# Graph stage: mask, shift, comparison and outputs as products of 32 columns, the centre's share as three bf16 parts

## The chip, the cores and the metric

One core of a Trainium2 chip runs the kernel. It has a matrix engine (TensorE, PE in the profile; its weight loads are PEld), VectorE (DVE), ScalarE (ACT), GpSimd (POOL) and SyncE (SP), which issues the DMAs. The metric is the device time of one execution in microseconds (us), as the median of several runs.

## What is computed

The reference is one layer of a small perceiver: a point cloud network over a context, whose result is added to `x`, a state space layer ("scan"), and a low rank feed forward layer. The change touches the first. For each of 16 batches there are 512 nodes with 32 features, ordered in four ways along space filling curves. In each order a node has a window of K = 10 neighbours. What matters here, cut from the reference:

```python
def _get_graph_features(feats, inds_list, perm, W_lin, b_lin, k=K):
    ...
    for inds in inds_list:
        neigh = gather(feats, inds)
        gf = jnp.concatenate([jnp.broadcast_to(center, (B, N, k, C)), neigh - center], axis=-1)
    ...
    x16 = x.astype(jnp.float16).astype(jnp.float32)
    qh = x16.reshape(B * N, k, nheads, headdim)
    scores = jnp.einsum('bihd,bjhd->bhij', qh, qh) / np.float32(np.sqrt(headdim))
    attn = jax.nn.softmax(scores, axis=-1)
    out = jnp.einsum('bhij,bjhd->bihd', attn, qh).reshape(B * N, k, total)
    fused = out @ W_lin.T + b_lin
...
g1 = _get_graph_features(f0, inds_list, perm1, W_lin1, b_lin1)
h1 = _lrelu(_instance_norm(jnp.einsum('oc,bnkc->bonk', W_conv1, g1), (2, 3)))
feats1 = h1.max(axis=-1)
g2 = _get_graph_features(feats1.transpose(0, 2, 1), inds_list, perm2, W_lin2, b_lin2)
h2 = _lrelu(_instance_norm(jnp.einsum('oc,bnkc->bonk', W_conv2, g2), (2, 3)))
feats2 = h2.max(axis=-1)
```

Layer 1 has 32 output channels, layer 2 has 64. The centre's half of the features is the same for all ten rows of a window, so its share of the output is one vector per node (`hc`), added to what attention gives of the differences to the neighbours.

## The kernel before

The kernel has three stages one behind the other: the graph stage (`graph_part`), the scan and the feed forward layer. The graph stage first makes the space filling keys and the first ranks, then runs eight blocks, `order` at L1026: four groups of four batches (128 partitions: four batches by 32 channels), each in layer 1 and in layer 2, as (group, layer) = (0,1), (1,1), (0,2), (2,1), (1,2), (3,1), (2,2), (3,2). A block has 43 iterations of 12 nodes, 344 in all. Layer 1 has one output tile of 128 partitions (`npair` 1), layer 2 two (`npair` 2).

The order of the instructions in this stage is written out by hand (`manual_schedule`, and the loop at L1074), as a pipeline over iterations. In iteration `it` TensorE receives, in this order:

- `expo` of the iteration before: a product of the identity `idb` with the negated row maxima `c` ("shift", L870), which adds to the scores in PSUM; ScalarE then takes the exponential (L875).
- `scores`: first the mask, a product of `mL` and `mR` that opens the accumulation in the PSUM tile `s` (L846), then 16 products of 32 columns (L853).
- perhaps a rank step: `compare`, a product of 128 columns by 512 (L540), whose signs ScalarE sums (L541). There are 256, 64 of them before the blocks, 64 each in the first, second and fourth block.
- `mapped`: 48 products of 32 columns by 128 (layer 1) or 256 (layer 2) that apply the weights, three bf16 parts of them (L915); ScalarE copies the result to `us` (L920).
- perhaps a step of `prep` for the next block, of which the largest on TensorE is `place`, twelve products of 32 columns by 512 (L705), 16 times per block.
- `outputs` of three iterations before: 16 f32 products that apply the attention weights `e` to `us` (L943). Each has `co` columns, 32 in layer 1 and 64 in layer 2; an f32 product is two instructions on TensorE, and every product has a weight load of its own. They go to the PSUM tile `h`, of which there is one buffer; it gathers four iterations in layer 1 and two in layer 2. In layer 1 a first f32 product of the identity and `hc` (L933) puts the centre's share in.

VectorE receives `turn` (a transpose, L896), `rest` and `reduce` (maximum and moments of `h`, L966 and L969; in layer 2 after an add of the centre's share at L960, which also frees `h`, with part of the reductions put off to the next iteration as `rest`), `greatest` (row maxima, L862), `sums` (L882), the one-hot rows of `prep` (L751) and the reciprocal in `shares` (L888). GpSimd makes the differences to the neighbours six iterations ahead (L811) and multiplies by the reciprocal (L890). SyncE issues the copies of those differences (`DX`, L821) and the loads and stores of `prep`.

`prep` is a generator, advanced by `steps` once or twice per iteration while the block before runs; `PREP` is the number of steps it is taken to have. Within it `share` makes `hc`: f16 rounding of the features, an f32 product per output tile (L666), and a copy with bias on ScalarE (L667).

Of the kernel before, what the change touches and what calls it, by code (L numbers as in the profile page):

```python
# [8 lines left out]
F32 = mybir.dt.float32  # L9
F16 = mybir.dt.float16  # L10
BF16 = mybir.dt.bfloat16
I32 = mybir.dt.int32
AF = mybir.ActivationFunctionType
ALU = mybir.AluOpType
AX = mybir.AxisListType
# [3 lines left out]
P = 128  # L19
B = 16  # L20
C = 32
D = 512
NBG = 4
M = 4
K = 10
NG = 12
NGRP = -(-D // NG)
NB = 3
QB = NB * K
NJ = NG // NB  # L30
NI = NJ * 4
# [14 lines left out]
NHT = 16  # L46
LR = 18
LEAD = 6
PREP = (49, 46, 42)
SPARE = 3  # L50


# [325 lines left out]
def graph_part(nc, tc, cx, I, dram, id32, ones, xt, F0, layernorm_steps, rstd_steps, scan_input):  # L378
# [10 lines left out]
    start = ExitStack()  # L389
# [14 lines left out]
    for L, co in ((1, 32), (2, 64)):  # L404
        for n, shape in (("wlA", [64, P]), ("wlC", [64, P]), ("wcT", [64, co]), ("bl", [64, 1])):
            t = wp.tile(shape, F32, name=f"{n}{L}")
            nc.sync.dma_start(out=t, in_=I[f"{n}{L}"])
            loaded[n, L] = t
    for dst, v, at in ((own, -1.0, (0, 4)), (others, 1.0, (2, 7))):
        t = kp.tile([M * B, D], BF16, name=f"sign{at[0]}")  # L410
# [12 lines left out]
    layers = []  # L423
# [8 lines left out]
    for k in range(2):  # L432
        kl = keep.tile([P, M, D], BF16, name=f"kl{k}")
# [23 lines left out]
    NQ = NG * K  # L457
# [21 lines left out]
    nc.scalar.copy(idb, id32)  # L479
    nid = kp.tile([P, P], BF16, name="nid")  # L480
    nc.scalar.mul(nid, id32, -1.0)
    orders = node_orders(nc, kp, kt, kps, X, idx, id32, nid, own, others)


# [52 lines left out]
    def compare(t, b, c, m):  # L537

        kl, kr = KS[b % 2]
        nc.tensor.matmul(t, lhsT=kl[:, m, c * P:(c + 1) * P], rhs=kr, start=True, stop=True)  # L540
        nc.scalar.activation(sgn, t, AF.Sign, accum_out=rank[:, c, m, b:b + 1])  # L541

    ranked = [0]
# [83 lines left out]
    def prep(g, layer, early=False):  # L627
# [26 lines left out]
        def share():  # L654

            c16 = wk.tile([P, D], F16, tag="c16", name=f"c16{key}", bufs=1)
            nc.vector.tensor_copy(c16, src)
            yield
            c32 = wk.tile([P, D], F32, tag="c32", name=f"c32{key}", bufs=1)
            nc.vector.tensor_copy(c32, c16)  # L660
            yield
            yield
            hc = wk.tile([P, npair, D], F32, tag="hc", name=f"hc{key}")
            for pr in range(npair):
                ph = ps_1.tile([P, D], F32, tag="misc", bufs=2, name=f"ph{key}_{pr}")
                nc.tensor.matmul(ph, lhsT=WC[:, pr], rhs=c32, start=True, stop=True)  # L666
                nc.scalar.activation(hc[:, pr], ph, AF.Identity, bias=HB)  # L667
                yield
            made[key][2] = hc

# [170 lines left out]
    def scores(at, gi):  # L841

        slot, c1 = at_piece(at, gi)
        d, dx = DD[slot], DX[slot]
        s = ps_s.tile([P, 512], F32, tag="s", name=f"s{at}_{gi}")[:, :NI * QB]
        nc.tensor.matmul(  # L846
            s, lhsT=mL.rearrange("p i q -> p (i q)"), rhs=mR, start=True, stop=False, skip_group_check=True
        )
        for j in range(NJ):
            c0 = c1 + j * QB  # L850
            for h in range(4):
                rh = slice(32 * h, 32 * h + 32)
                nc.tensor.matmul(  # L853
                    s[rh, j * 4 * QB:(j + 1) * 4 * QB].rearrange("p (b q) -> p b q", b=4),
                    lhsT=d[:, h, c0:c0 + 32], rhs=dx[:, h, :, c0:c0 + QB],
                    start=False, stop=(j == NJ - 1), skip_group_check=True,
                )
        live["s", at, gi] = s
# [8 lines left out]
    def expo(at, gi):  # L867

        s, c = live.pop(("s", at, gi)), live.pop(("c", at, gi))
        nc.tensor.matmul(  # L870
            s, lhsT=idb, rhs=c.unsqueeze(2).to_broadcast([P, NI, QB]), start=False, stop=True,
            skip_group_check=True,
        )
        e = sm.tile([P, NI, QB], F32, tag="e1", name=f"e1{at}_{gi}", bufs=3)
        nc.scalar.activation(e, s.rearrange("p (i q) -> p i q", q=QB), AF.Exp, scale=smc)  # L875
        live["e1", at, gi] = e
# [46 lines left out]
    def outputs(at, gi):  # L923
        key, co, npair, WA, hc, per = state[at][:6]
        us, e = live.pop(("us", at, gi)), live.pop(("e2", at, gi))
        slot = gi % per
        if slot == 0:
            live["h", at] = ps_1.tile([P, npair, per * NQ], F32, tag="h", name=f"h{at}_{gi}")
            if npair == 1:

                f0 = gi * NG
                nn = min(f0 + per * NG, D) - f0
                nc.tensor.matmul(  # L933
                    live["h", at][:, 0, :nn * K].rearrange("p (n j) -> p n j", j=K), lhsT=id32,
                    rhs=hc[:, 0, f0:f0 + nn].unsqueeze(2).to_broadcast([P, nn, K]), start=True, stop=False,
                    skip_group_check=True,
                )
        h = live["h", at]
        for j in range(NJ):
            for b in range(4):  # L940
                pr, r = divmod(b * co, P)
                q0 = slot * NQ + j * QB
                nc.tensor.matmul(  # L943
                    h[r:r + co, pr, q0:q0 + QB], lhsT=us[:, j, b * co:(b + 1) * co],
                    rhs=e[:, 4 * j + b, :QB], start=npair > 1, stop=True, skip_group_check=True,
                )
        if slot == per - 1 or gi == NGRP - 1:
            live["full", at, gi] = h

    def reduce(at, gi):  # L950
        key, co, npair, WA, hc, per, mxo, stats = state[at]
        h = live.pop(("full", at, gi), None)
        if h is None:
            return
        f0 = (gi - gi % per) * NG
        nn = min((gi + 1) * NG, D) - f0
        hs = h[:, :, :nn * K].rearrange("p r (n j) -> p r n j", j=K)
        if layers[order[at][1]][0] == 2:
            t = sm.tile([P, npair, per * NG, K], F32, tag="hs", name=f"hs{at}_{gi}", bufs=1)
            nc.vector.tensor_tensor(  # L960
                t[:, :, :nn], hs, hc[:, :, f0:f0 + nn].unsqueeze(3).to_broadcast([P, npair, nn, K]), ALU.add,
            )
            hs = t[:, :, :nn]

        def greatest_of():
            nc.vector.tensor_reduce(mxo[:, :, f0:f0 + nn], hs, AX.X, ALU.max)  # L966

        def moments(pr):
            nc.vector.bn_stats(stats[:, pr, gi // per], hs[:, pr].rearrange("p n j -> p (n j)"))  # L969

        if npair == 1:
            greatest_of()
            moments(0)
        else:
            moments(0)
            live["rest", at] = lambda: (greatest_of(), moments(1))
        if gi == NGRP - 1:
            rest(at, gi)
            tails.append(end(at))

    def rest(at, gi):
        if ("rest", at) in live:
            live.pop(("rest", at))()

    def end(at):

# [24 lines left out]
    def finish(g, F2):  # L1011
        p3 = ps_1.tile([P, D], F32, tag="misc", bufs=2, name=f"p3_{g}")
        for j, f in enumerate((F0[:, g], F1[g], *F2)):
            nc.tensor.matmul(p3, lhsT=W3[:, j], rhs=f, start=(j == 0), stop=(j == 3))
        h3 = wk.tile([P, D], F32, tag="h3", name=f"h3_{g}", bufs=1)
        nc.scalar.copy(h3, p3)
        yield
        n3 = wk.tile([P, D], F32, tag="n3", name=f"n3_{g}", bufs=1)
        yield from layernorm_steps(sm, n3, h3, f"f{g}")
        yield  # L1020
        nc.vector.scalar_tensor_tensor(n3, n3, 0.2, n3, ALU.mult, ALU.max)
        yield
        nc.vector.tensor_tensor(xt[:, g], xt[:, g], n3, ALU.add)
# [50 lines left out]
    for it in range(len(blocks) + 5):  # L1074

        def do(step, lag):
            if 0 <= it - lag < len(blocks):
                step(*blocks[it - lag])

        at, gi = blocks[it] if it < len(blocks) else (len(order), 0)  # L1080
        if gi == 0 and it < len(blocks):
            begin(at)
        do(expo, 1)
        for oh, of in transfers:
            nc.scalar.dma_start(out=oh, in_=of)
        transfers.clear()
        do(turn, 3)
        do(scores, 0)
        do(rest, 5)
        do(reduce, 4)  # L1090
        if ranked[0] < wanted(at):
            rank_step(later_tile)
        do(greatest, 0)
        do(mapped, 0)
        do(sums, 1)
        if at + 1 == len(order) and gi == 4:
            tails.extend(scan_input(sm, junk(q), q) for q in range(NBG - 1))
        steps(at, gi)
        do(shares, 1)
        if ranked[0] < wanted(at) and (at == 0 or gi % 2):  # L1100
            rank_step(later_tile)
        do(outputs, 3)
        if at == 0 and gi < 8:
            rank_step(later_tile)
        if it + LEAD < len(blocks):
            to, g2 = blocks[it + LEAD]
            if g2 == 0:
                for _ in ahead[to][0]:
                    pass
            differences(to, g2)  # L1110
# [551 lines left out]
```

## Time and profile before

| | us |
|---|---|
| median of 3 runs | 2316.69 (2315.12 to 2320.33) |
| span of the profiled execution | 2316.7 |
| stage before the blocks | 0 to 93.8 |
| layer 1 blocks (first, second, fourth, sixth) | 155.9, 142.6, 146.5, 144.7 |
| layer 2 blocks (third, fifth, seventh, eighth) | 153.8, 153.8, 151.3, 144.6 |
| scan and feed forward, from the end of the last block | about 1030 |

A block is counted from the first mask product (L846) of its first iteration to that of the next block. The lines below are from the list of instruction groups with shapes kept apart: line, engine, operation, tiles written and read, shape and count, then busy us and mean ns of one, then idle time of the engine ahead of them and what ended it.

```profile
L943 PE MATMUL h<-e,us 128*64 128x30 f32 x5504 | 194.3, 223 | 9.6 <-DVE hs L960 6.1 <-DVE e L896 2.7 <-issue 0.3
...
L870 PE MATMUL s<-c,idb 128*128 128x480 bf16 x344 | 130.4, 379 | 5.6 <-DVE c L862 2.7 <-DVE e L896 1.5 <-DVE z L882 0.8
L846 PE MATMUL s<-mR,mL 128*128 128x480 bf16 x344 | 127.0, 369 | 0.0
L705 PE MATMUL pp<-oh,F 128*32 128x512 bf16 x1536 | 109.5, 380 | 3.4 <-ACT so L712 1.5 <-issue 1.1 <-DVE oh L751 0.6
L540 PE MATMUL kd<-kr,kl 128*128 128x512 bf16 x256 | 104.6, 424 | 4.8 <-DMA kr<-others 1.0 <-ACT sgn L541 0.5 <-issue 0.3
...
L943 PE MATMUL h<-e,us 128*32 128x30 f32 x5504 | 84.9, 197 | 21.7 <-issue 13.7 <-DVE e L896 7.4
...
L960 DVE TENSOR_TENSOR hs<-h,hc 128x480 f32<-128x480 f32 x84 | 53.3, 635 | 14.1 <-PE h L943 14.1
```

In a product's form, 128*32 means 128 rows and 32 columns of the array; 128x480 is what moves through it. The mean of one product is its latency, since products run into each other; for what one costs, starts have to be compared. "issue" names idle time for which the profile shows no other engine.

### The profile page before, as it was taken

The page shows a single profiled execution, that of the slowest core. Times are in us where ns is not written, and L with a number is a line of the kernel's source. Part 1 is how long each engine was busy: PE and PEld are TensorE (multiplying, and loading weights), DVE is VectorE, ACT ScalarE, POOL GpSimd, SP SyncE. Part 2 cuts the span into 40 slices and gives each one's busy share as a digit, 9 for nine tenths or more (in the row PEclk, how much of TensorE's full clock was granted, in tenths as well). Part 3 has the DMA queues.
Part 4 walks back from the last instruction along what each step waited for, and adds up shares of the span by engine and source line. Part 5 has one row for each costly group of instructions (what it writes and reads, how often), then busy time and mean ns, then how long its engine had stood idle before and what let it go on. Part 6 is the DMA issues. An engine that isn't in the chain of part 4 may idle for free. (4 is left out here: it accounts for less than half of the span.)

```text
span 2316.7 us, 89754 instructions
## 1 busy us (share of the span) xinstructions
PE 2131.8 (92%) x39522; PEld 1300.3 (56%) x39522; DVE 1835.5 (79%) x3974; ACT 1140.4 (49%) x2073; POOL 840.7 (36%) x897
## 2 busy tenths in 40 slices
PE   5599899999999998899999789989999999999979
PEld 2255555776557775567777544455646566464422
DVE  8488897999989999889999763788786967866643
ACT  6686667556675554455555222433353534435321
POOL 2156656455565565655655100111120202112200
PEclk9899999999999999999999799999999999999989
DMA  1324242231232322323212112112122121211100
GB/s 46 81 59 84 52 81 60 52 83 45 63 76 48 82 52 49 84 47 77 56 36 44 49 51 79 60 56 89 45 73 64 46 91 55 73 60 46 37 37 18
DMA packets 121629, 138.05 MB, mean 60 GB/s; under 512 B 18398, under 2 KB 79506, under 8 KB 121154
## 3 DMA queue, kind: packets, MB, share of 16 engines
q1 hardware_dynamic: 121240, 132.32, 22.5%
q8 instruction: 311, 5.10, 1.0%
q14 instruction: 78, 0.64, 0.1%
HBM read 77.02 MB, written 12.85 MB: 39 GB/s over the span
## 5 line engine op out<-in xcount | busy, mean ns | idle before, releaser
L890 POOL TENSOR_TENSOR EN<-e,rz 128x480 f32<-128x480 f32 x344 | 342.5, 996 | 499.4 <-DVE rz L888 410.2
L915 PE MATMUL u<-WA,DD 128*32 128x128 bf16 (+1 forms) x16512 | 414.1, 248 | 16.6 <-issue 16.4
L920 ACT COPY us<-u 128x512 f32<-128x512 f32 x516 | 302.1, 587 | 152.3 <-PE u L915 136.9
L915 PEld LDWEIGHTS <-DD 128*32 128x32 f16 x16512 | 338.6, 97 | 50.6 <-issue 48.1
L875 ACT ACTIVATE e<-s,smc 128x480 f32<-128x480 f32 x344 | 227.7, 662 | 252.6 <-PE s L870 222.0
L811 POOL TENSOR_TENSOR DD<-fs,crep 128x480 f16<-128x480 f32 (+2 forms) x344 | 349.6, 1017 | 0.0
L943 PEld LDWEIGHTS h<-e,us 128*32 128x32 f32 (+1 forms) x11008 | 246.0, 125 | 133.4 <-issue 66.6
L943 PE MATMUL h<-e,us 128*32 128x30 f32 (+1 forms) x11008 | 279.2, 210 | 31.3 <-issue 14.0
L1368 POOL TENSOR_TENSOR ssq<-ssq,sq 128x512 f32<-128x512 f32 x56 | 89.9, 1606 | 592.6 <-ACT sq L1367 592.6
L862 DVE TENSOR_REDUCE c<-s 128x16 bf16<-128x480 f32 x344 | 220.5, 641 | 83.8 <-PE s L853 80.4
L1181 PE MATMUL ppg<-hT,wing 128*128 128x512 f32 x512 | 238.3, 609 | 0.0
L1181 PE MATMUL ppch<-hT,winch 128*128 128x512 f32 x512 | 230.5, 592 | 0.0
L896 DVE STREAM_TRANSPOSE e<-EN 128x512 f32<-128x512 f32 x344 | 224.7, 653 | 0.0
L882 DVE TENSOR_REDUCE z<-e 128x16 f32<-128x480 f32 x344 | 219.6, 638 | 0.5 <-ACT e L875 0.4
L1194 DVE SCALAR_TENSOR_TENSOR cyh<-ppch,t_conv_w,cyh 128x496 f32<-128x496 f32 (+2 forms) x192 | 137.5, 716 | 99.9 <-ACT cyh L1188 95.3
L541 ACT ACTIVATE sgn<-kd 128x512 bf16<-128x512 f32 x256 | 153.1, 598 | 51.4 <-PE kd L540 48.3
L853 PEld LDWEIGHTS <-DD 128*32 128x32 f16 x5504 | 80.8, 96 | 158.2 <-issue 135.5
L751 DVE TENSOR_SCALAR oh<-it,rank 128x512 bf16<-128x512 f16 x512 | 155.8, 365 | 8.5 <-PE pp L705 8.5
L853 PE MATMUL s<-DX,DD 128*32 128x120 f16 x5504 | 142.3, 221 | 18.6 <-DMA DX<-DD 15.3
L1181 PEld LDWEIGHTS ppch<-hT,winch 128*128 128x128 f32 x512 | 94.5, 190 | 109.1 <-issue 102.5
L1181 PEld LDWEIGHTS ppg<-hT,wing 128*128 128x128 f32 x512 | 94.5, 192 | 107.0 <-issue 99.4
L870 PE MATMUL s<-c,idb 128*128 128x480 bf16 x344 | 130.4, 379 | 5.6 <-DVE c L862 2.7
(372 smaller groups left out, 3156.1 us busy)
## 6 DMA issues: line engine op xcount, KB each, us to landing
DX<-DD SPq DMA_DIRECT2D x456, 90.0 KB
wing<-in_in_proj SPq DMA_DIRECT2D x64, 256.0 KB
winch<-in_in_proj SPq DMA_DIRECT2D x64, 256.0 KB
wo<-in_out_proj SPq DMA_DIRECT2D x64, 256.0 KB
crep<-dC SPq DMA_DIRECT2D x128, 64.0 KB
dS<-so SPq DMA_DIRECT2D x32, 256.0 KB
fs<-dS SPq DMA_DIRECT2D x128, 64.0 KB
wincB<-in_in_proj SPq DMA_DIRECT2D x8, 256.0 KB
```

Of the source, the lines that this page charges most:

```text
L751: nc.vector.tensor_scalar(oh[:, j], it2, rank[:, c, m, 4 * g + b:4 * g + b + 1], None, ALU.is_equal)
L811: nc.gpsimd.tensor_tensor(d[:, :, m0 - n0:n1 - n0], win, crep[:, :, m0:n1].unsqueeze(3).to_broadcast([P, 4, n1 - m0, K]), ALU.subtract,)
L853: nc.tensor.matmul(s[rh, j * 4 * QB:(j + 1) * 4 * QB].rearrange("p (b q) -> p b q", b=4), lhsT=d[:, h, c0:c0 + 32], rhs=dx[:, h, :, c0:c0 ...
L862: nc.vector.tensor_reduce(c, live["s", at, gi].rearrange("p (i q) -> p i q", q=QB), AX.X, ALU.max, negate=True)
L875: nc.scalar.activation(e, s.rearrange("p (i q) -> p i q", q=QB), AF.Exp, scale=smc)
L882: nc.vector.tensor_reduce(z, e, AX.X, ALU.add)
L890: nc.gpsimd.tensor_tensor(en[:, :, :QB], e, rz.unsqueeze(2).to_broadcast([P, NI, QB]), ALU.mult)
L896: nc.vector.transpose(e.rearrange("p i q -> p (i q)"), en.rearrange("p i q -> p (i q)"))
L915: nc.tensor.matmul(u[rh, jj], lhsT=d[:, h, c0:c0 + 32], rhs=WA[k][:, h].rearrange("p b o -> p (b o)"), start=(jj == 0 and k == 0), stop=(k ...
L920: nc.scalar.copy(us[:, j - jj:j + 1], u)
L943: nc.tensor.matmul(h[r:r + co, pr, q0:q0 + QB], lhsT=us[:, j, b * co:(b + 1) * co], rhs=e[:, 4 * j + b, :QB], start=npair > 1, stop=True, ...
L1181: nc.tensor.matmul(pp, lhsT=w[:, k], rhs=hT[:, k], start=(k == 0), stop=(k == 3))
```

## The change

Four products of the whole width become four products of 32 columns each, in a helper `bands`: the comparison, the mask, the shift, and the centre's share. The outputs of layer 2 become twice as many products of 32 columns in place of 64. The centre's share enters `h` by TensorE in both layers, as three bf16 parts in place of one f32 product; the parts are made in `share` by ScalarE and GpSimd. In layer 2 the add on VectorE falls away, the reductions read `h` in PSUM, and all of them stand in `reduce`; `rest` is gone. `PREP` follows the number of steps; three work tiles share buffers with others.

```diff
-PREP = (49, 46, 42)
+PREP = (52, 52, 42)
...
+    def bands(t, lhs_of, rhs, start, stop):
+
+        for r in range(4):
+            rr = slice(32 * r, 32 * r + 32)
+            nc.tensor.matmul(t[rr], lhsT=lhs_of(r, rr), rhs=rhs, start=start, stop=stop, skip_group_check=True)
...
     def compare(t, b, c, m):
-        nc.tensor.matmul(t, lhsT=kl[:, m, c * P:(c + 1) * P], rhs=kr, start=True, stop=True)
+        bands(t, lambda r, rr: kl[:, m, c * P + 32 * r:c * P + 32 * r + 32], kr, True, True)
...
-            c32 = wk.tile([P, D], F32, tag="c32", name=f"c32{key}", bufs=1)
+            c32 = wk.tile([P, D], F32, tag="FT", name=f"c32{key}", bufs=1)
...
-            hc = wk.tile([P, npair, D], F32, tag="hc", name=f"hc{key}")
+            hc = wk.tile([P, 3, npair, D], BF16, tag="hc", name=f"hc{key}")
             for pr in range(npair):
                 ph = ps_1.tile([P, D], F32, tag="misc", bufs=2, name=f"ph{key}_{pr}")
                 nc.tensor.matmul(ph, lhsT=WC[:, pr], rhs=c32, start=True, stop=True)
-                nc.scalar.activation(hc[:, pr], ph, AF.Identity, bias=HB)
+                whole = wk.tile([P, D], F32, tag="whole", name=f"whole{key}_{pr}", bufs=1)
+                nc.scalar.activation(whole, ph, AF.Identity, bias=HB)
+                yield
+                for k in range(3):
+                    nc.scalar.copy(hc[:, k, pr], whole)
+                    if k < 2:
+                        nc.gpsimd.tensor_tensor(whole, whole, hc[:, k, pr], ALU.subtract)
+                        yield
                 yield
...
-        nc.tensor.matmul(
-            s, lhsT=mL.rearrange("p i q -> p (i q)"), rhs=mR, start=True, stop=False, skip_group_check=True
-        )
+        bands(s, lambda r, rr: mL[:, r], mR, True, False)
...
-        nc.tensor.matmul(
-            s, lhsT=idb, rhs=c.unsqueeze(2).to_broadcast([P, NI, QB]), start=False, stop=True,
-            skip_group_check=True,
-        )
+        bands(s, lambda r, rr: idb[:, rr], c.unsqueeze(2).to_broadcast([P, NI, QB]), False, True)
...
-            if npair == 1:
-
-                f0 = gi * NG
-                nn = min(f0 + per * NG, D) - f0
-                nc.tensor.matmul(
-                    live["h", at][:, 0, :nn * K].rearrange("p (n j) -> p n j", j=K), lhsT=id32,
-                    rhs=hc[:, 0, f0:f0 + nn].unsqueeze(2).to_broadcast([P, nn, K]), start=True, stop=False,
-                    skip_group_check=True,
+            f0 = gi * NG
+            nn = min(f0 + per * NG, D) - f0
+            for k in range(3):
+                bands(
+                    live["h", at][:, :, :nn * K].rearrange("p r (n j) -> p r n j", j=K), lambda r, rr: idb[:, rr],
+                    hc[:, k, :, f0:f0 + nn].unsqueeze(3).to_broadcast([P, npair, nn, K]), k == 0, False,
                 )
         h = live["h", at]
         for j in range(NJ):
-            for b in range(4):
-                pr, r = divmod(b * co, P)
-                q0 = slot * NQ + j * QB
+            q0 = slot * NQ + j * QB
+            for o in range(0, 4 * co, 32):
+                pr, r = divmod(o, P)
                 nc.tensor.matmul(
-                    h[r:r + co, pr, q0:q0 + QB], lhsT=us[:, j, b * co:(b + 1) * co],
-                    rhs=e[:, 4 * j + b, :QB], start=npair > 1, stop=True, skip_group_check=True,
+                    h[r:r + 32, pr, q0:q0 + QB], lhsT=us[:, j, o:o + 32],
+                    rhs=e[:, 4 * j + o // co, :QB], start=False, stop=True, skip_group_check=True,
                 )
...
-        if layers[order[at][1]][0] == 2:
-            t = sm.tile([P, npair, per * NG, K], F32, tag="hs", name=f"hs{at}_{gi}", bufs=1)
-            nc.vector.tensor_tensor(
-                t[:, :, :nn], hs, hc[:, :, f0:f0 + nn].unsqueeze(3).to_broadcast([P, npair, nn, K]), ALU.add,
-            )
-            hs = t[:, :, :nn]
...
+        nc.vector.tensor_reduce(mxo[:, :, f0:f0 + nn], hs, AX.X, ALU.max)
+        for pr in range(npair):
             nc.vector.bn_stats(stats[:, pr, gi // per], hs[:, pr].rearrange("p n j -> p (n j)"))
...
-        do(rest, 5)
```

More of the change, by code (lines that the diff above doesn't have):

```diff
@@ L957, in reduce @@
         hs = h[:, :, :nn * K].rearrange("p r (n j) -> p r n j", j=K)
-        if layers[order[at][1]][0] == 2:
-            t = sm.tile([P, npair, per * NG, K], F32, tag="hs", name=f"hs{at}_{gi}", bufs=1)
-            nc.vector.tensor_tensor(
-                t[:, :, :nn], hs, hc[:, :, f0:f0 + nn].unsqueeze(3).to_broadcast([P, npair, nn, K]), ALU.add,
-            )
-            hs = t[:, :, :nn]
-        def greatest_of():
-            nc.vector.tensor_reduce(mxo[:, :, f0:f0 + nn], hs, AX.X, ALU.max)
-        def moments(pr):
-            nc.vector.bn_stats(stats[:, pr, gi // per], hs[:, pr].rearrange("p n j -> p (n j)"))
[L971 to L976, printed above, removed]
+        nc.vector.tensor_reduce(mxo[:, :, f0:f0 + nn], hs, AX.X, ALU.max)
+        for pr in range(npair):
+            nc.vector.bn_stats(stats[:, pr, gi // per], hs[:, pr].rearrange("p n j -> p (n j)"))
         if gi == NGRP - 1:
-            rest(at, gi)
             tails.append(end(at))
-    def rest(at, gi):
-        if ("rest", at) in live:
-            live.pop(("rest", at))()
     def end(at):
@@ L1017, in finish @@
         yield
-        n3 = wk.tile([P, D], F32, tag="n3", name=f"n3_{g}", bufs=1)
+        n3 = wk.tile([P, D], F32, tag="lr", name=f"n3_{g}", bufs=1)
         yield from layernorm_steps(sm, n3, h3, f"f{g}")
```

## The prediction

> **What bounds the kernel now.** I read the engines' busy shares first, then the same shares for each of the eight blocks of the graph stage, then TensorE's timeline inside one layer 2 block and one layer 1 block, then the DMA queues and the stalls of TensorE that no other engine ends. The chain of waits only followed the run's last 87 us, far behind the change, so it says nothing here.
>
> ```profile
> PE 2131.8 (92%) x39522; PEld 1300.3 (56%) x39522; DVE 1835.5 (79%) x3974; ACT 1140.4 (49%) x2073; POOL 840.7 (36%) x897
> ...
> q8 instruction: 311, 5.10, 1.0%
> ```
>
> TensorE leads. The queue line matters more than its 1.0% suggests: 5.10 MB over TensorE's 2 x 39522 instructions is 64.5 bytes each, so q8 is TensorE's own program arriving, 311 packets of 16.4 KB, about 256 instructions (128 pairs of weight load and product) in each.
>
> ```profile
> 392.30:546.10 153.80, 150.85 (x4416) 115.38 (x4414) 144.16 (x342) 83.22 (x140) 87.24 (x96) 0.99 0.27 60
> ...
> 846.40:991.10 144.70, 118.08 (x4444) 75.81 (x4442) 130.37 (x301) 59.16 (x100) 86.94 (x97) 0.96 0.28 63
> ```
>
> The columns are the stretch, its length, and busy us of TensorE, weight loads, VectorE, ScalarE and GpSimd, then clock and DMA. The first row is a layer 2 block: TensorE busy 150.85 of 153.80 us. The second is the layer 1 block without comparisons: only 118.08 of 144.70. A steady layer 2 iteration:
>
> ```profile
> 1103.65 0.38 PE L870 MATMUL s<-c,idb 128*128 128x480 bf16 x1
> 1103.87 0.37 PE L846 MATMUL s<-mR,mL 128*128 128x480 bf16 x1
> 1104.16 0.40 PE L853 MATMUL s<-DX,DD 128*32 128x120 f16 x16
> 1104.39 1.48 PE L915 MATMUL u<-WA,DD 128*32 128x256 bf16 x48
> 1105.80 1.12 PE L943 MATMUL h<-e,us 128*64 128x30 f32 x32
> 1106.86 0.38 PE L870 MATMUL s<-c,idb 128*128 128x480 bf16 x1
> ```
>
> From start to start: shift 0.213, mask 0.296, scores 0.229, map 1.416, outputs 1.056, in all 3.21 us (three digits are medians over all iterations). Each step between widths costs: the map takes 1.309 us ahead of other 32 column products and 1.416 ahead of the 64 column outputs; the scores take 0.229 ahead of the map and 0.337 ahead of a comparison; mask to scores is 0.296 and shift to mask 0.213. So narrowing the array costs about 0.085 us and widening 0.105 us. That is what the change removes.
>
> But in layer 1 TensorE stops with nothing to wait for:
>
> ```profile
> 961.52 0.36 PE L943 MATMUL h<-e,us 128*32 128x30 f32 x24
> 963.93 0.27 PE L943 MATMUL h<-e,us 128*32 128x30 f32 x8 [2.05 <-issue]
> ...
> 966.66 0.22 PE L915 MATMUL u<-WA,DD 128*32 128x128 bf16 x3
> 968.07 0.83 PE L915 MATMUL u<-WA,DD 128*32 128x128 bf16 x45 [1.19 <-issue]
> ```
>
> The stops fall in the middle of a loop of equal products, at no fixed instruction. The trace's q8 packets began at 960.79, 965.47 and 969.60 us. TensorE resumes at 963.93 and 968.07: about 3.1 and 2.6 us behind a packet's start, and the next packet starts 1.5 us behind each resumption. I collected every such stop over 0.3 us in the eight blocks: 40. From packet start to resumption 2.2 to 3.5 us, from resumption to the next packet 1.0 to 1.8, packet to packet 3.37 to 4.69, median 3.84, tenth percentile 3.47. So a packet is asked for when TensorE enters the one before, and with one under way at a time TensorE cannot run more than 256 instructions per round trip. No stretch of 1024 instructions in the trace is faster than 3.41 us per 256, none of 4096 faster than 3.71. A layer 2 iteration has 98 pairs, 196 instructions in 3.21 us, or 4.19 us per 256: just inside.
>
> **The change part by part.** TensorE's work, in us of array time. A 480 column product as four bands: L705 puts twelve 32 column products of 512 columns through in 0.648 us, three for each of the four column groups, so four run beside each other and 480 columns cost 0.203; the map gives 0.205. I take 0.205 (bounds: 0.20, and 0.82 if the bands went one by one, which no 32 column row shows).
>
> Layer 2 outputs become 64 products of exactly the form that layer 1 has (32 columns, 30 moving, f32). Layer 1 takes 0.389 us for 32 with a widening behind them, 0.284 without, so 64 take 0.57 against 1.056 (upper bound: 64 column rows' 33 ns each, 2.1). The centre's share in layer 2 adds 3 x 0.205 per two iterations, 0.31 each. Layer 2: 0.205 + 0.205 + 0.229 + 1.309 + 0.57 + 0.31 = 2.82 us against 3.21. Layer 1 with comparison and placement: 0.213 + 0.296 + 0.337 + 0.320 + 0.680 + 0.648 + 0.389 = 2.88 becomes 0.205 + 0.205 + 0.229 + 0.219 + 0.680 + 0.648 + 0.284 = 2.47; its centre's share goes from two f32 halves (1.0 us with the step before) to 0.62 per four iterations.
>
> VectorE loses 84 adds at L960 (53.3 us). Its three reductions now read the one PSUM tile `h`: 0.53 + 2 x 0.31 from start to start, 1.16 us, where the add held it 0.65. The next block of `h`, now begun by the centre's product, waits for that behind shift, mask, scores and map (1.95 us): 0.8 us of cover. If it went, TensorE with the next expo behind it would stand still for the excess at most every second iteration. ScalarE gains 36 copies of 0.587 us, 21 us over eight blocks in which it idles over 40 us each; GpSimd gains 24 subtractions between 1.0 (L890) and 1.6 us (L1368), 24 to 38 us, against idle time above 50 us per block. These lie some 40 steps ahead of their use; uncovered, they would be about 5 us a pair, 60 in all. I cost both at nothing. Preparation takes 3 or 6 steps more; at worst a flush of a few us per block. No DMA moves.
>
> Now the instructions. Added pairs in the blocks: mask and shift 344 x 6 = 2064; comparisons 192 x 3 = 576 (64 run before); centre, layer 1, 44 x 10 = 440; centre, layer 2, 88 x 12 = 1056; outputs, layer 2, 172 x 32 = 5504. Together 9640 pairs, 19280 instructions, 75.3 packets. The blocks hold 276 packets now, so 351.3. Array time per 256 in layer 2 falls to 2.82 us / 284 x 256 = 2.54, plus placements about 2.8: below any round trip seen. Layer 1 with 240 instructions in 2.47 us is at 2.63. So the round trip decides all eight blocks. I take 3.75 us: the stopped intervals' median 3.84 is biased to slow packets (mean packet 1.24 us there, 1.15 over the stage), and the dense stretch at 216 to 254 us shows 3.75. Then 351.3 x 3.75 = 1317, plus the 15.3 us that TensorE waits for the first load of DX at L853, 1333. The eight blocks take 1193.2 now, so +140. Nothing outside them changes: before them packets are over 13 us apart, from 1310 us on over 20. The profiled span is 2316.7 and the runs' median 2316.69, so 2316.7 + 140 = 2457 us.
>
> The bounds: 3.47 gives 1219 + 15, +41, 2358; the stretch at 941 to 992 us, 3.95 on average, gives 1388 + 15 and 10 for other waits, +220, 2537.
>
> The Trainium skill speaks against this sum. "Runtime: NRT & Kernel Launch", section "Instruction fetch mechanics", has the same 256 instruction blocks fetched while the current one executes, but calls the cost of crossing a boundary mostly hidden and gives TensorE room for 2048 instructions. By it the supply is free and the sum is the first rival's below. The 40 stops show otherwise here.
>
> **The rivals.** First, faster: supply keeps up and the removed steps between widths count. For it: layer 2 blocks are 98% TensorE now. Layer 2 at -0.39 us x 172 gives -66; layer 1 at 0.19 x 172 + 0.20 x 192 + 0.38 x 44 = -88, halved, since VectorE, busy 117 to 130 of 143 to 156 us, fills up: -44. 2207 us. It needs a round trip below (1193.2 - 15.3) / 351.3 = 3.35 us, the point from which the sign turns; only one of the 40 packet distances came near it, at 3.37. Chance 0.10.
>
> Second, slower by the array itself: narrow outputs cost as much each as the 64 column ones, 64 x 33 ns = 2.11. A layer 2 iteration would be 4.37, +1.16 x 172 = +199, less layer 1's 44: 2472. Against it stands layer 1's row of the same form. Chance 0.04; the time hardly differs, the stops would.
>
> Third, the single `h`: the reductions outlast their cover by, say, 0.5 us on 86 + 44 groups, +65 on top of the first rival's -110: 2272. VectorE's 144 of 154 us speak for it, its 53 us of relief against. Chance 0.02.
>
> **How the numbers follow.** Forecast 0.84: 2457, range 2360 to 2540 from the two bounds; the rivals with other times hold 0.12 outside it, the ends of the round trip the rest. Below 0.2% (5 us) a measurement of this kernel can't tell a difference. Faster 0.10, same 0.03 (a round trip within 3.33 to 3.37, or rivals that cancel), slower 0.87.
>
> **What would show it.** Right: q8 at about 388 packets and 3.5 to 3.9 us apart through all blocks, layer 2 included; TensorE's stops named "issue" up from 36 us to some 300; its busy share in layer 2 down from 98% to near 75%; VectorE and ScalarE waiting for TensorE; steps shift to mask to scores near 0.2 us each; layer 2 iterations near 4.2 us. Wrong: layer 2 iterations of 2.8 to 3.0 us, packets nearer than 3.3 us, or long waits of the centre's product for the reductions.

## The result, and the profile after

The changed kernel takes 2511.93 us (2509.09 to 2515.22, 4 runs) against 2318.51 for the kernel before in the same runs: a ratio of 1.0831, 95% interval 1.0815 to 1.0847. It is slower by 193 us. TensorE's mean granted clock is the same in the two profiled executions, 0.977 before and 0.978 after. The time lies inside the forecast's range; the forecast itself, 2457, is 55 us short.

The engines' busy shares and the queue line of the changed kernel, as shown of before:

```profile
PE 2036.3 (81%) x49354; PEld 1361.3 (54%) x49354; DVE 1801.6 (72%) x3886; ACT 1145.7 (46%) x2109; POOL 867.2 (35%) x921
...
q8 instruction: 387, 6.34, 1.1%
```

TensorE has 9832 pairs more and is busy 95 us less: the array work did shrink. All engines have a lower share of a longer span. The queue that brings TensorE's program has 387 packets in place of 311.

The busy time by block, two blocks of the changed kernel (the third, layer 2, and the sixth, layer 1), with the columns as before; a block is counted here and below from the first row maximum (`greatest`) of its first iteration to that of the next block, and the last block to its last output products, within 2 us (the 144.6 us of the last block in the table of before end 8 us earlier, at its last mask):

```profile
428.60:616.30 187.70, 144.00 (x6234) 122.38 (x6235) 134.78 (x324) 85.11 (x143) 89.09 (x98) 0.99 0.23 50
...
962.60:1113.30 150.70, 104.63 (x4886) 78.30 (x4884) 132.28 (x297) 61.65 (x106) 90.28 (x99) 0.99 0.29 61
```

Counted so, the same layer 2 block before:

```profile
393.90:547.00 153.10, 150.15 (x4383) 114.61 (x4381) 143.43 (x341) 82.81 (x139) 86.69 (x96) 0.99 0.27 60
```

It took 153.1 us with TensorE busy 150.2. Now it takes 187.7 with TensorE busy 144.0: 77%, and no other engine is above 72%. All eight blocks went from 1185.2 to 1372.6 us, +187.4. The rest of the span's +192.4 is 6.4 us before the first block and -1.4 behind the last.

TensorE's timeline in a layer 2 iteration of the changed kernel:

```profile
1203.42 0.41 PE L487 MATMUL s<-mR,mL 128*32 128x480 bf16 x4
1203.62 0.43 PE L865 MATMUL s<-DX,DD 128*32 128x120 f16 x16
1203.84 1.51 PE L924 MATMUL u<-WA,DD 128*32 128x256 bf16 x48
1205.15 0.85 PE L719 MATMUL pp<-oh,F 128*32 128x512 bf16 x12
1205.80 0.32 PE L950 MATMUL h<-e,us 128*32 128x30 f32 x12
1206.99 0.62 PE L950 MATMUL h<-e,us 128*32 128x30 f32 x50 [0.87 <-issue]
```

Each step costs what the change meant it to: four bands of the mask 0.20 us, scores 0.22 with no switch behind them, map 1.31, placement 0.65. Then TensorE stops for 0.87 us between two equal output products, and no engine is named. The costliest TensorE groups of the graph stage show where such stops fell over the whole run (busy, mean, then idle time ahead and what ended it):

```profile
L924 PE MATMUL u<-WA,DD 128*32 128x256 bf16 x8256 | 278.4, 274 | 66.4 <-issue 63.9 <-ACT us L929 2.3
L950 PE MATMUL h<-e,us 128*32 128x30 f32 x16512 | 245.6, 196 | 134.2 <-issue 126.9 <-DVE e L905 6.5
...
L924 PE MATMUL u<-WA,DD 128*32 128x128 bf16 x8256 | 165.0, 224 | 60.6 <-issue 60.6
L865 PE MATMUL s<-DX,DD 128*32 128x120 f16 x5504 | 157.1, 219 | 61.1 <-issue 43.7 <-DMA DX<-DD 16.9 <-POOL DD L825 0.3
```

"issue" leads in each of these groups, with 7.3 to 7.9 ns for each of its products: a stop hits whatever product comes next when a packet runs out. Two VectorE groups of the same kernel show the other side:

```profile
L874 DVE TENSOR_REDUCE c<-s 128x16 bf16<-128x480 f32 x344 | 221.9, 645 | 211.5 <-PE s L865 211.0
...
L965 DVE TENSOR_REDUCE mxo<-h 128x48 f32<-128x480 f32 (+1 forms) x132 | 82.8, 627 | 72.0 <-PE h L950 71.8
```

The first of them before:

```profile
L862 DVE TENSOR_REDUCE c<-s 128x16 bf16<-128x480 f32 x344 | 220.5, 641 | 83.8 <-PE s L853 80.4
```

VectorE waits 211 us for the scores (80.4 before) and 71.8 us for `h`. It is TensorE that is late, not the reductions that hold `h`: the centre's products wait for the moments (L967) 10.5 us in all, and TensorE's waits for VectorE to free `h` were 16.4 us before.

The trace has 294 stops of TensorE above 0.3 us in the blocks that end by "issue"; before, 40. From a q8 packet's start to the resumption 2.58 us on average (the packet itself 1.18), from there to the next packet's start 1.30, packet to packet 3.88.

The places of the stops agree with the packets. Counted in TensorE's own instructions, weight loads included, every one of the 294 after the first lies a multiple of 256 behind the one before it, to within two instructions, and 252 lie exactly 256 behind. A limit on the rate of single products or weight loads would not stop TensorE once in 256 instructions, at whatever product stands there.

### The profile page after: what moved, and what is told of

The parts are those of the page before. It is cut to its first block, busy times and chain, and to the rows that moved or that the text cites. A ratio compares the mean times of both kernels' runs of the same rounds, so it can differ in the third digit from the quotient of the medians.

```text
span 2509.0 us, 109348 instructions
## 1 busy us (share of the span) xinstructions
PE 2036.3 (81%) x49354; PEld 1361.3 (54%) x49354; DVE 1801.6 (72%) x3886; ACT 1145.7 (46%) x2109; POOL 867.2 (35%) x921
## 3 DMA queue, kind: packets, MB, share of 16 engines
q1 hardware_dynamic: 121240, 132.32, 21.0%
## 5 line engine op out<-in xcount | busy, mean ns | idle before, releaser
L924 PE MATMUL u<-WA,DD 128*32 128x128 bf16 (+1 forms) x16512 | 443.5, 249 | 126.9 <-issue 124.5
L924 PEld LDWEIGHTS <-DD 128*32 128x32 f16 x16512 | 366.4, 98 | 164.8 <-issue 155.9
L950 PE MATMUL h<-e,us 128*32 128x30 f32 x16512 | 245.6, 196 | 134.2 <-issue 126.9
L950 PEld LDWEIGHTS h<-e,us 128*32 128x32 f32 x16512 | 233.7, 111 | 184.0 <-issue 140.5
L865 PE MATMUL s<-DX,DD 128*32 128x120 f16 x5504 | 157.1, 219 | 61.1 <-issue 43.7
L865 PEld LDWEIGHTS <-DD 128*32 128x32 f16 x5504 | 134.9, 97 | 113.3 <-issue 47.5
L487 PE MATMUL s<-mR,mL 128*32 128x480 bf16 x1376 | 147.2, 370 | 16.3 <-issue 11.4
```

The costliest lines, as they stand in the source:

```text
L865: nc.tensor.matmul(s[rh, j * 4 * QB:(j + 1) * 4 * QB].rearrange("p (b q) -> p b q", b=4), lhsT=d[:, h, c0:c0 + 32], rhs=dx[:, h, :, c0:c0 ...
L924: nc.tensor.matmul(u[rh, jj], lhsT=d[:, h, c0:c0 + 32], rhs=WA[k][:, h].rearrange("p b o -> p (b o)"), start=(jj == 0 and k == 0), stop=(k ...
L950: nc.tensor.matmul(h[r:r + 32, pr, q0:q0 + QB], lhsT=us[:, j, o:o + 32], rhs=e[:, 4 * j + o // co, :QB], start=False, stop=True, skip_grou ...
```

## The experiments

Two theories. **Supply**: TensorE's program arrives 256 instructions at a time, each packet asked for when the one before begins, so 256 instructions take at least one round trip, about 3.9 us. **Array**: the new products, their waits or the reductions are what costs, and the number of instructions is free. All ratios are against the kernel before in the same runs (2315.69 us for e1 to e4, 2313.41 for the others).

| run | us | ratio to before, 95% interval |
|---|---|---|
| e1, before with 44 empty pairs per layer 2 iteration | 2451.33 | 1.0599 (1.0575 to 1.0624) |
| e2, change with a short map in layer 2 | 2487.94 | 1.0759 (1.0732 to 1.0785) |
| e3, change with wide outputs | 2382.73 | 1.0303 (1.0274 to 1.0332) |
| e4, before with mask, shift, comparison in bands | 2328.19 | 1.0073 (1.0045 to 1.0100) |
| e5, change without the copies to DX | 2454.83 | 1.0615 (1.0591 to 1.0639) |
| e6, before with a map of two parts | 2261.88 | 0.9780 (0.9759 to 0.9802) |
| e7, change with a map of two parts | 2364.11 | 1.0223 (1.0199 to 1.0246) |
| e9, before with a short map in layer 1 | 2311.07 | 0.9992 (0.9980 to 1.0004) |

**e1: instructions alone.** To the kernel before, at the end of `scores` (`s512` is the whole PSUM tile of 512 columns, `s` its first 480):

```diff
+        if order[at][1]:
+            for n in range(44):
+                rr = slice(32 * (n % 4), 32 * (n % 4) + 32)
+                nc.tensor.matmul(
+                    s512[rr, NI * QB:NI * QB + 2], lhsT=idb[:, rr], rhs=mR[:, :2], start=False, stop=True,
+                    skip_group_check=True,
+                )
```

> The kernel before, with 44 pairs of weight load and product more in each layer 2 iteration, so that a layer 2 block has as many TensorE instructions as in the changed kernel (about 12630). Each product moves 2 columns into PSUM columns that nobody reads. Supply theory (one packet of 256 instructions per round trip of 3.9 us): 12630 / 256 x 3.9 = 192 us per layer 2 block in place of 152, +160 us, 2477 us, with packets 3.8 to 4.0 us apart in layer 2. Array theory (the changed kernel is slower because its products, waits or reductions cost more, and instructions are free): 44 x 8.5 ns of array time at most, +64 us, 2381 us, or no change at all.

Measured 2451 us, +136. The busy time by block, fourth (layer 1, nothing added) and fifth (layer 2):

```profile
578.30:725.60 147.30, 138.97 (x4569) 79.93 (x4571) 130.90 (x301) 101.00 (x228) 85.83 (x95) 0.99 0.29 65
725.60:911.70 186.10, 170.40 (x6286) 130.59 (x6278) 146.81 (x342) 83.25 (x139) 86.70 (x96) 1.00 0.23 52
```

The layer 1 block stays at its 147.3 us. The four layer 2 blocks take 187.8, 186.1, 190.0 and 182.1 us; in the changed kernel they take 187.7, 185.0, 185.5 and 190.4. Products that compute nothing, as many as the change adds, reproduce its layer 2: 746.0 us in all against 748.6, with single blocks up to 8 us apart. Yet the array steps of an iteration add up to some 3.5 us here (an estimate, 3.21 + 0.33) and to 2.8 in the changed kernel. The timeline shows that it isn't their array time:

```profile
906.93 0.41 PE L854 MATMUL s<-DX,DD 128*32 128x120 f16 x16
907.16 0.39 PE L862 MATMUL s<-mR,idb 128*32 128x2 bf16 x31
907.96 0.25 PE L862 MATMUL s<-mR,idb 128*32 128x2 bf16 x13 [0.42 <-issue]
```

Undisturbed, all 44 take 0.33 us (903.16 to 903.49 in the same timeline), which over 172 iterations makes 57 of the 136 us at most. Here TensorE runs dry in the middle of them.

**e2: less array time, same instructions.** In the changed kernel's `mapped`:

```diff
+                w = 32 if k and npair == 2 else 4 * co
...
-                        u[rh, jj], lhsT=d[:, h, c0:c0 + 32], rhs=WA[k][:, h].rearrange("p b o -> p (b o)"),
+                        u[rh, jj, :w], lhsT=d[:, h, c0:c0 + 32],
+                        rhs=WA[k][:, h].rearrange("p b o -> p (b o)")[:, :w],
```

> The changed kernel, with the second and third weight part of layer 2's map moving 32 columns in place of 256 (it leaves out seven eighths of these two parts). Same number of instructions, 0.76 us less array time per layer 2 iteration. Supply theory: nothing is gained, 2505 to 2515 us, the idle time of TensorE grows instead. Array theory: -0.76 x 172 = -131 us, 2381 us.

Measured 2488, below the 2505 to 2515 of the supply theory and far above the 2381 of the other. Of 131 us of array time taken out, 24 came back, and 17 of them in layer 2's blocks (183, 181, 181 and 187 us in place of 188, 185, 186 and 190); the packets there came 3.74 to 3.79 us apart in place of 3.81 to 3.88. Why they came a little nearer wasn't settled. The timeline, where the map is now short:

```profile
1201.49 0.41 PE L865 MATMUL s<-DX,DD 128*32 128x120 f16 x15
1203.74 0.21 PE L865 MATMUL s<-DX,DD 128*32 128x120 f16 x1 [1.83 <-issue]
1203.74 0.81 PE L925 MATMUL u<-WA,DD 128*32 128x256 bf16 x47
```

The map takes 0.66 us in place of 1.31, and the stop grows to 1.83: what is saved is waited for.

**e3: more array time, fewer instructions.** The changed kernel with one part undone, in `outputs`:

```diff
-            for o in range(0, 4 * co, 32):
-                pr, r = divmod(o, P)
+            for b in range(4):
+                pr, r = divmod(b * co, P)
                 nc.tensor.matmul(
-                    h[r:r + 32, pr, q0:q0 + QB], lhsT=us[:, j, o:o + 32],
-                    rhs=e[:, 4 * j + o // co, :QB], start=False, stop=True, skip_group_check=True,
+                    h[r:r + co, pr, q0:q0 + QB], lhsT=us[:, j, b * co:(b + 1) * co],
+                    rhs=e[:, 4 * j + b, :QB], start=False, stop=True, skip_group_check=True,
                 )
```

> The changed kernel with layer 2's outputs back at 64 columns: 2752 instructions less per layer 2 block, and 0.6 us more array time per iteration. Supply theory: 9740 / 256 x 3.9 = 148 us of supply, so the array decides again with about 3.46 us an iteration, 164 us a block against 187: -92 us, 2420 us. Array theory: 0.49 to 0.6 us x 172 more, 2590 us or above.

Measured 2383, 129 us less than the change: layer 2's blocks take 162.4, 160.4, 161.8 and 154.7 us, and their "issue" stops fall from over 40 us to 4.1 or less each. The third block, with TensorE busy again for nearly all of it:

```profile
420.30:582.70 162.40, 157.15 (x4941) 125.39 (x4943) 134.57 (x323) 84.70 (x143) 89.04 (x98) 1.00 0.26 57
```

So two thirds of the loss belong to the outputs of layer 2 alone, which the array does faster in their new form. It is below the 2420 expected, because layer 2 came out 3 us a block shorter and layer 1, with the same instructions as in the change, at 607 us in place of 624: its packets came 3.89 to 3.95 us apart in this execution and 3.90 to 4.03 in the change's. The round trip differs by some per cent between executions.

**e4: bands alone.** The helper and the three places (mask, shift, comparison) put into the kernel before, by the lines of the diff above.

> The kernel before with mask, shift and comparison alone as four products of 32 columns. Supply theory: layer 1, already at its round trips, gets 500 to 900 instructions more per block, +32 us in all; layer 2 is let off 0.19 us of array time per iteration but comes to the supply limit at 143 us, -14 us: together 2335 us, a little slower. Array theory: -0.19 us x 344 and -0.2 us x 192 in part, 2250 us.

Measured 2328, +12.5. Layer 1's blocks went from 575.9 to 594.2 us, layer 2's from 609.3 to 599.7. Both signs are those of the supply theory (+32 and -14 expected): removing the switches between widths pays in layer 2, where the array decided, and costs more than it pays in layer 1, where instructions do.

**e5: the other transfers.** The changed kernel without the DMAs in `differences`:

```diff
-            for b in range(4):
-                rb = slice(32 * b, 32 * b + 32)
-                nc.sync.dma_start(out=DX[slot][rb, :, b, cols], in_=DD[slot][rb, :, cols])
+            pass
```

> The changed kernel without the copies of the differences from DD to DX (456 DMAs of 90 KB); the scores are then products with zeros, so the attention is left out. Same instructions on TensorE. If the round trip of 3.9 us is made longer by other transfers on the same 16 DMA engines, its packets fall from 1.18 us to the 0.95 us of the quiet stretches, distances to about 3.65 us: 352 x -0.25 = -88 us, and -17 us for the first wait for DX: 2405 us. If the round trip doesn't depend on them, only the first wait goes: 2495 us.

Measured 2455, between the two numbers. The queue lines of this kernel:

```profile
q1 hardware_dynamic: 54424, 89.89, 13.8%
q8 instruction: 386, 6.32, 1.1%
```

Over half of the other packets are gone (121240 before), and within the blocks four fifths (15760 in place of 81815). The eight blocks take 1316 us, 56 less, 0.16 us for each of some 350 packets. Part of that can be the difference between executions: e2, with all the copies, had packets of 1.12 us as this one has (1.18 in the change's execution), and layer 2 distances only 0.09 below the change's. But the changed kernel's own trace shows the same size: in layer 2 the distances average 3.75 us where other transfers kept the DMA engines under 5% busy from one packet to the next, and 3.96 where over 30%. So the other transfers make up 0.1 to 0.2 us of the round trip, and over 3.6 us of it stay without most of them.

**e9: layer 1 before the change.** The edit of e2 in the kernel before, for `npair == 1`.

> The kernel before with the second and third weight part of layer 1's map moving 32 columns in place of 128 (it leaves out three quarters of these two parts): same instructions, 0.33 us less array time per layer 1 iteration. If layer 1 of the kernel before is already at its round trips: -10 us at most, 2305 to 2317 us. If its array time decides: -0.33 x 172 = -56 us, 2260 us.

Measured 2311 against 2313; the interval of the ratio includes 1. The sixth block, before and here:

```profile
847.30:992.10 144.80, 118.18 (x4446) 75.90 (x4438) 130.51 (x301) 59.16 (x100) 86.62 (x96) 0.96 0.28 63
840.20:982.70 142.50, 106.66 (x4438) 67.15 (x4425) 130.84 (x302) 58.86 (x100) 86.50 (x96) 0.99 0.31 64
```

The array time of layer 1's map falls by a third of a microsecond per iteration and next to nothing is gained: TensorE's "issue" stops in the four layer 1 blocks double from 33 to 66 us, and their length falls by 9 us. VectorE, busy 130.5 of 144.8 us in the sixth block, would be the other bound; but e6 below leaves its work as it is, takes instructions away, and brings that block to 137.5 us. So layer 1 was at its supply limit already. That is why the saving of 0.4 us per iteration, which the change brings there, could not show.

**e6 and e7: fewer instructions.** The map's weights as two f16 parts of 11 bits in place of three bf16 parts of 8, scaled so that the second part stays in range; e6 in the kernel before, e7 in the changed one:

```diff
-        WA = [gc.tile([P, 4, 4, co], BF16, name=f"WA{L}_{k}") for k in range(3)]
+        WA = [gc.tile([P, 4, 4, co], F16, name=f"WA{L}_{k}") for k in range(2)]
...
+        ws = wp.tile([64, co], F32, name=f"wts{L}")
+        nc.scalar.mul(ws, wt, 8192.0)
...
-            for k in range(3):
+            for k in range(2):
...
-                nc.scalar.copy(us[:, j - jj:j + 1], u)
+                nc.scalar.mul(us[:, j - jj:j + 1], u, 1.0 / 8192.0)
```

> The kernel before with the map's weights as two f16 parts (scaled by 8192, undone in the copy to us) in place of three bf16 parts: 16 pairs less per iteration, 1376 instructions per block, and less array time by 0.22 us (layer 1) and 0.43 us (layer 2). Supply theory: layer 1 comes off its round trips (7700 / 256 x 3.85 = 116 us) to VectorE's 113 to 122 us of work plus waits, about 128 us a block; layer 2 comes to VectorE's 141 us, about 145 us: together -85 us, 2230 us. Array theory: layer 1 has no supply limit and its 9 us of waits stay, -0.22 x 172 = -38 us at most there, layer 2 as above: 2255 us.

> The changed kernel with the map's weights as two f16 parts. Supply theory: layer 2 has 11110 instructions a block, 43.4 x 3.85 = 167 us against 187, layer 1 about 8700, 34 x 3.85 = 131, with waits 136, against 156: 160 us less, 2352 us. It stays slower than the kernel before although its array time per layer 2 iteration, 2.4 us, is far below the 3.21 of before. Array theory: -0.43 x 172 - 0.22 x 172 = -112 us, 2400 us.

e7: 2364 us, as the supply theory had it within 12. Its layer 2 iteration has 2.4 us of array time against the 3.21 of before, and the kernel is still slower than before. e6: 2262 us, faster than both kernels, by 2.2% than before; the supply theory had 2230 and the array theory 2255, so its time alone does not tell them apart. Layer 2's blocks came out as expected (144 to 145 us, 148.8 the last), layer 1's took 130 to 143 in place of 128. They are 29 us shorter in all than before, where e9, with more array time taken away and no instruction, came to 9. TensorE groups of e6:

```profile
L945 PE MATMUL h<-e,us 128*64 128x30 f32 x5504 | 193.6, 223 | 44.2 <-DVE hs L962 32.4 <-DVE e L898 10.7 <-DVE stats L971 0.2
...
L935 PE MATMUL h<-hc,id 128*128 128x480 f32 x80 | 43.5, 628 | 22.9 <-DVE stats L971 20.8 <-DVE hs L962 1.7
```

The stops have names again: TensorE now waits for VectorE, in layer 2 for the add that frees `h`, in layer 1 for the moments that read it. With 267 packets the supply is nearly out of the way (14.9 us of "issue" are left at layer 1's map and 7.4 at its outputs) and VectorE is the next bound.

## Why the prediction held, point by point

**What bounds the kernel.** Right, and the experiments show it rather than the correlation alone: instructions without work cost layer 2 as much as the change's do (e1), and array work taken away without instructions saves little where packets decide (24 of 131 us in e2, 2 of 56 in e9).

**Array terms.** Right to a few hundredths: from start to start and without stops, shift 0.202 us, mask 0.202, scores 0.217 (0.205, 0.205, 0.229 forecast), map 1.309, the centre's share 0.607 per two iterations, 64 narrow outputs 0.52 to 0.56 (0.57 forecast).

**Instructions.** 387 packets where 388 were forecast; some 352 in the blocks against 351.3.

**The round trip.** This is the term that was mis-sized. The prediction took 3.75 us: the stopped intervals' median of 3.84, set down as biased to slow packets. In the changed kernel, where nearly every packet is waited for, the distance over the blocks is 1372.6 / 352 = 3.90 us on average, and 351.3 x 0.15 = 53 us. The blocks came out 47 us above their forecast (+187.4 against +140), so this term covers all of that; the 6 us between are about a packet and a half, and lie in where the blocks' ends are counted. The rest of the 55 us is 5 outside the blocks and some 3 between the profiled execution and the median. The ground for the discount was not all wrong: packets at the stops are shorter now (1.18 us against 1.24), and the median distance did fall, to 3.80. But a sum over packets needs their mean, and that hardly moved: 3.89 at the 40 stops of before, 3.88 at the 294.

**What was costed at nothing.** The wait for `h`, the steps added to `prep` and ScalarE's copies did stay hidden in the blocks. Not so ahead of the first, where the prediction expected no change: its `prep` has no block in front of it, and the parts of the centre's share (three copies and two subtractions in turn) run in the open. The first placement starts at 76.50 us in place of 71.11, and the first copy to DX is issued at 111.69 in place of 105.34. From there to the first scores it is 4.1 us in both kernels, so the first row maximum comes 6.4 us later.

**The rivals.** The faster case needed a round trip below 3.35 us; the nearest packets in the whole changed kernel are 3.29 apart, the average 3.9. Costly narrow outputs are refuted by their row. The single `h` costs 10.5 us of waits in all, less than the 16.4 of before.

## What to carry to other kernels

Count TensorE's instructions per iteration as well as its array time: in these runs they arrived in packets of 256, weight loads included, at least 3.2 us apart, and 3.9 on average in the changed kernel: 30 ns for each weight load with its product. Shorter runs of products go through much faster (e1's 44 in 0.33 us), so a short timeline doesn't show the limit. A form that is faster in the array but needs more products is a loss when it stands near that rate; TensorE stopping in the middle of a row of equal products, with no engine named, is the sign, and the count and the distances of the instruction packets, and stops that lie 256 instructions apart, confirm it. Where it binds, take instructions away (in e6 and e7 a third of the map's), and even at more array time, as e3 shows.

## What the runs showed of the hardware

The supply of instructions as a bound was forecast; that it had already bound layer 1's blocks, a quarter of the kernel before, was not, though the prediction shows their stops. Layer 1's blocks ran at packets 3.9 to 4.0 us apart in the median, and removing a third of a microsecond of array work per iteration (e9) took 9 us off them in place of 56. The round trip depends little on the load on the DMA engines: with a fifth of the other packets in the blocks (e5) it fell by 0.16 of 3.9 us at most. What makes up the other 3.7 us stays open. Stepping to a wider form of products cost 0.105 us and to a narrower one 0.085 in the kernel before, and in the changed kernel, where all neighbours have 32 columns, neither is seen.
